# Rearranging the last four units of a fused attention and gated-FFN kernel

## The chip, the cores and the metric

The kernel runs on one core of a Trainium2 chip. The metric is the device time of one execution in microseconds; the median of several runs is compared. All data are float32.

## The reference

Input `x` is 8 x 256 x 512 (2048 tokens of 512). Two pre-norm blocks follow each other:

```python
x = x + attn(layernorm(x), w_qkv, w_o)
x = x + ffn(layernorm(x), weight, bias, centroids, assignments)
```

Attention has 32 query heads and 8 key/value heads of 128, is causal, and adds a bias of `-slope(head) * sqrt(distance)` to the scores. The FFN is one dense layer of 512 x 512 that is masked by token and by column:

```python
dots = softmax(x @ centroids.T / 0.1)     # 64 clusters
hits = dots > 0.01
query_sel = any(hits, axis=1)             # one flag for each token
row_sel = any(hits, axis=0)[assignments]  # one flag for each output column
out = where(query_sel & row_sel, x @ weight.T + bias, 0)
```

The column flags need the hits of every token. So no output can be written before the last token has its hits.

## The kernel before

The 2048 tokens are 16 tiles of 128, in four pairs of sequences (`p`, four tiles each). A unit `u` of the main loop is one sequence of a pair and one key/value head with its four query heads; there are `NU` = 64 units, 16 (`SPP`) for each pair. The loop runs to `u` = 65, since the work is spread over three units: unit `u` makes the scores and the maxima over keys of `u`, the exponentials and sums of `u - 1`, and P @ v and the output projection of `u - 2`.

The order on every engine is written out by hand (a manual schedule): each engine works through its instructions in program order, and a helper such as `av(0)` or `f(1)` puts its instructions on the engines where it is called. These are the helpers that the change touches:

- `scores`, `over_keys`, `over_quadrants` (behind `rows` and `rows_max`): the scores are made with keys on partitions, so maxima and sums over keys need a reduction in DVE (`r`), a transpose on PE (`tp_r`), another reduction (`row`), and two DMAs on the SP queue: `row` to memory and from there, broadcast, to `bc`. `subtract_max` (POOL for the first 1024 columns, DVE for the rest) and `attend` read `bc`.
- `av(i)` is P @ v of unit `u - 2` (two half products, scaled by 1/sum into `oT` by DVE), and behind the second half POOL makes the four sums of `oT` for a Strassen scheme.
- `w(i)` is product `i` of that scheme for the output projection. Products 1, 6, 7 and 4 add up in one bank (`ps_oa`), and each has to be read (by ACT into `snap`, or by DVE) before the next adds into it. The parts in `snap` are added into the residual `x2` on POOL by `flush_adds`, at the start of the next unit. The last unit (`direct`) adds from the bank on DVE.
- `norm(0)` to `norm(3)`: statistics (DVE), square root (ACT), scale and shift (DVE), normalised tile (ACT) of two tiles.
- `f(0)` to `f(3)` are the FFN of a tile `t_ffn`: transposes of the normalised tile and a copy (`xnT`), the product (`ffn_both`: columns 256 to 575 with the 64 logits, and columns 0 to 255), maximum and exponential of the logits, the bias, and the hits, token flag and residual. Tiles 8 to 11 have it in units 62 to 65, tiles 12 to 15 (`last` = 12) behind the loop.

In unit 65 and behind the loop the last four tiles are normalised as their residuals get ready. `hits_any` gathers the hits; `cnt` and `rsel` are the two products that make the column flags of them. Then DVE puts `y` over `x` where the flag is set (`copy_predicated`) tile by tile, and the SP and ACT queues store in turn. Tiles 1, 2 and 3 (`SPLIT`) are done by POOL with a multiplication and an addition. Finished tiles 0 to 7 had been put aside in memory and are loaded again as four transfers of 1 MB (`back`), at the end of unit 63.

Tiles of a pool with a tag share `bufs` buffers: `p_tp` (transposes) has one bank, `p_sc` two, `p_acc` three, `p_long` one for each of its two tags.

Of the kernel before, what the change touches and what calls it, by code (L numbers as in the profile page):

```python
# [14 lines left out]
F32 = mybir.dt.float32  # L15
I32 = mybir.dt.int32
# [5 lines left out]
B, S, H = 8, 256, 512  # L22
# [31 lines left out]
def block_kernel(  # L54
# [463 lines left out]
    def ffn_logits_product(t, w_ffn):  # L518
        lg = p_sc.tile([P, 512], F32, tag="sc", name="lg")
        ffn_product(t, w_ffn, H, NCL, lg)  # L520
        ffn_sb[t] = lg[:, :NCL]

    def ffn_dense(t, w_ffn, chunks=range(NC_H)):
        if 0 in chunks:
            y_sb[t] = [p_acc.tile([P, 512], F32, tag="acc", name="ps_f")]
        ffn_product(t, w_ffn, 0, H, y_sb[t][0], chunks)

    def ffn_both(t, w_ffn):

        second = p_sc.tile([P, 512], F32, tag="sc", name="ps_lg")  # L530
        ffn_product(t, w_ffn, HH, HH + NCL, second)
        first = p_acc.tile([P, 512], F32, tag="acc", name="ps_f")
        ffn_product(t, w_ffn, 0, HH, first)
        ffn_sb[t] = second[:, HH : HH + NCL]
        y_sb[t] = [first[:, :HH], second[:, :HH]]
# [114 lines left out]
    for u in range(NU + 2):  # L650
# [46 lines left out]
        def f(part):  # L697
            if t_ffn is not None:
                if part == 0:
                    ffn_transpose(t_ffn)  # L700
                elif part == 1:
                    ffn_both(t_ffn, w_ffn)
                    ffn_max(t_ffn)
                    ffn_exp(t_ffn)
                elif part == 2:
                    ffn_bias_add(t_ffn, y_late[:, t_ffn % TPP, :] if t_ffn >= first_late else None)
                else:
                    ffn_hits(t_ffn)
                    ffn_qsel(t_ffn)
                    ffn_end(t_ffn)  # L710
# [3 lines left out]
        if more_p and slot in (10, 11):  # L714
            t_norm = (p + 1) * TPP + 2 * (slot - 10)
        elif own and p > 0 and slot in (2, 4) and p < NPAIR - 1:
            t_norm = (p - 1) * TPP + slot - 2
        elif u in (NU - 3, NU - 1):
            t_norm = (NPAIR - 2) * TPP + u - (NU - 3)

# [54 lines left out]
        if bb == 0 and own:  # L775
            qq(1), e(1), max_and_old(), e(2), f(0), av(0), e(6), exp_old(), av(1), more_sums(), rows_max(), f(1), e(7), qq(2)
# [4 lines left out]
        elif u < NU - 1:  # L781
            e(1), qq(4), e(2), max_and_old(), f(0), e(6), av(0), exp_old(), e(7), av(1), f(1), e(5), qq(5)
            f(2), norm(0), e(4), e(3), x(0), w(1), x(1), sum_old(), w(5, 6), norm(1), qq(3), w(2)
            rows(), behind_rows(), w(7, 3), norm(3), w(4)
        elif own:

            max_and_old(), f(0), av(0), exp_old(), av(1), rows_max(), f(1)
            f(2), norm(0), w(1), sum_old(), w(5, 6), norm(1), w(2)
            rows(), subtract_max(u, 0), subtract_max(u, 1)
            f(3), norm(2), w(7)  # L790
            nc.scalar.activation(s_sb[u], s_sb[u], AF.Exp)
            w(3), norm(3), w(4)
        elif bb == 0:
            sum_old(), av(0), av(1), f(0), rows(), f(1), w(1, 5), f(2), w(6, 2, 7, 3, 4), f(3)
        else:
            av(0), f(0), av(1), f(1)
            normalise(norm_stats(last, last + 1), tags=("y", "y"))
            ffn_hits(t_ffn), ffn_qsel(t_ffn)
            w(1), f(2), w(2, 5, 6)
            ffn_transpose(last)  # L800
            w(3)
            found = norm_root(norm_stats(last + 2))
            ffn_transpose(last + 1, "snap")
            w(7)
            norm_write(norm_scale(found))
            ffn_logits_product(last, w_ffn), ffn_logits_product(last + 1, w_ffn)
            w(4)

# [37 lines left out]
        if u == NU - 1:  # L846
# [12 lines left out]
    ffn_dense(last, w_ffn)  # L859
    normalise(norm_stats(last + 3))  # L860
    ffn_max(last), ffn_exp(last)
    ffn_max(last + 1), ffn_exp(last + 1)
    ffn_transpose(last + 2, copy=nc.vector.tensor_copy)
    ffn_transpose(last + 3, "o_s", tp=p_acc.tile([P, 512], F32, tag="acc", name="tpx_late"), copy=nc.vector.tensor_copy)
    ffn_logits_product(last + 2, w_ffn), ffn_logits_product(last + 3, w_ffn)
    ffn_max(last + 2), ffn_exp(last + 2)
    ffn_max(last + 3), ffn_exp(last + 3, work.tile([P, NCL], F32, tag="kT", name="e_last", bufs=2))
    ffn_dense(last + 1, w_ffn, (0, 1))
    for i in range(4):
        ffn_hits(last + i)  # L870
# [5 lines left out]
    nc.vector.tensor_scalar(csel, cnt[:NCL, :P], 0.0, None, ALU.is_gt)  # L876
    rsel = p_tp.tile([P, 512], F32, tag="tp", name="rsel")
    nc.tensor.matmul(rsel, lhsT=csel, rhs=onehot, start=True, stop=True)  # L878
    ffn_dense(last + 1, w_ffn, (2, 3))
# [6 lines left out]
    ffn_end(last - 1), ffn_bias_add(last, y_of(0)), ffn_end(last), ffn_qsel(last + 1)  # L886
    ffn_dense(last + 2, w_ffn)
    rsel_sb = work.tile([P, H], F32, tag="s", name="rsel_sb", bufs=3)
    nc.scalar.copy(rsel_sb, rsel)
    ffn_dense(last + 3, w_ffn)  # L890
    ffn_bias_add(last + 1, y_of(1)), ffn_end(last + 1)
# [5 lines left out]
    n = 0  # L897
    for t in range(NT):
        if t in SPLIT:
            continue  # L900
        p, i = divmod(t, TPP)
        if t >= last + 2:
# [7 lines left out]
        n += 1  # L910
# [23 lines left out]
```

## Time and profile before

| | |
|---|---|
| median of 3 runs | 1436.63 us (1436.61 to 1437.09) |
| profiled execution, its own time | 1438.62 us |
| its span, first to last instruction | 1436.8 us |
| busy: PE / DVE / POOL / ACT | 1404.8 / 928.7 / 877.6 / 372.4 us |
| mean granted clock of TensorE | 0.995 |
| DMA over the span | 190.20 MB, 132 GB/s |

Busy time is an average over the whole span. The change lies in its last 120 us, so the timeline of each engine there counts more than the shares. In a timeline line the columns are start, duration, engine, line of the kernel, operation, output and inputs; the bracket at the end holds the idle time ahead of it on its engine and the instruction that ended it. The timeline merges instructions of one kind. Matmuls in float32 appear as two records each, with weight loads as rows of their own.

### The profile page before, as it was taken

Reading aid. Unit: us, or ns where it says so; the run is one execution under the profiler, and the core shown is the slowest. Engines: PE = TensorE matmul, PEld = TensorE weight load, DVE = VectorE, ACT = ScalarE, POOL = GpSimd, SP = SyncE. Lnnn points to the kernel's source line nnn. Section 1 sums busy time; section 2 is a strip of 40 time slices with the busy share of each in tenths; the row PEclk is TensorE's granted clock in tenths of the full one; section 3 lists DMA queues with packets and bytes.
Section 4 is the critical chain, followed back from the end, with each engine's and each line's share of the span. In section 5 each row is a group of like instructions: output and inputs, shape, how many; then the busy total and the mean of one; then the engine's idle time right before and its main releaser. Section 6 shows DMA issues by size and latency. Waiting matters only on the chain. (4 is left out here: it accounts for less than half of the span.)

```text
span 1436.8 us, 16560 instructions
## 1 busy us (share of the span) xinstructions
PE 1404.8 (98%) x5859; PEld 1082.3 (75%) x5859; DVE 928.7 (65%) x1720; ACT 372.4 (26%) x650; POOL 877.6 (61%) x883
## 2 busy tenths in 40 slices
PE   8899999999999999999999999999999999999986
PEld 7677777767878777777778777787777777777663
DVE  5557656676566665667655666566756676556776
ACT  3222223411232222332213312142222221222332
POOL 6377857767465754667655466566747666466643
PEclk9999999999999999999999999999999999999998
DMA  5235433443242544424243424434323353243243
GB/s 187 94 117 177 132 117 133 147 147 125 96 165 74 176 147 148 162 96 142 101 147 107 171 87 169 168 112 148 132 100 107 132 176 132 90 165 103 91 160 117
DMA packets 87024, 190.20 MB, mean 132 GB/s; under 512 B 11648, under 2 KB 19840, under 8 KB 86944
## 3 DMA queue, kind: packets, MB, share of 16 engines
q1 hardware_dynamic: 85792, 186.67, 37.9%
q10 hardware_dynamic: 864, 1.57, 0.3%
q8 instruction: 47, 0.77, 0.2%
q0 software_dynamic: 288, 0.92, 0.2%
q14 instruction: 33, 0.27, 0.1%
HBM read 176.03 MB, written 13.11 MB: 132 GB/s over the span
## 5 line engine op out<-in xcount | busy, mean ns | idle before, releaser
L423 POOL TENSOR_TENSOR s<-s,bc 128x1024 f32<-128x1024 f32 x64 | 151.7, 2371 | 151.4 <-DMA bc<-row_hbm 151.3
L501 POOL TENSOR_TENSOR x<-x,snap 128x256 f32<-128x256 f32 x189 | 136.0, 735 | 172.1 <-DVE x L489 99.0
L388 DVE TRANSPOSE_TENSOR_REDUCE r<-s 128x32 f32<-128x1024 f32 x128 | 158.0, 1234 | 4.3 <-ACT s L740 4.3
L112 POOL TENSOR_TENSOR o_s<-oT 128x256 f32<-128x256 f32 x64 | 47.7, 745 | 184.3 <-DVE oT L451 178.8
L158 ACT COPY qT<-ps_qa 128x512 f32<-128x512 f32 x128 | 74.7, 583 | 287.4 <-PE ps_qa L145 287.3
L484 ACT COPY snap<-ps_oa 128x256 f32<-128x256 f32 x189 | 70.3, 372 | 274.6 <-PE ps_oa L469 274.6
L469 PE MATMUL ps_oa<-wo,oT 128*128 128x256 f32 x512 | 133.1, 382 | 2.7 <-DVE oT L451 2.7
L740 ACT ACTIVATE s<-s 128x1536 f32<-128x1536 f32 x63 | 93.5, 1484 | 149.3 <-DVE s L426 138.5
L447 PE MATMUL av<-s,v 128*128 128x512 f32 x256 | 130.7, 592 | 0.0
L145 PE MATMUL ps_qa<-xT,wq 128*128 128x256 f32 x512 | 121.1, 379 | 0.8 <-ACT qT L158 0.8
L371 PE MATMUL sc<-qT,kT 128*128 128x512 f32 x256 | 120.3, 592 | 0.0
L145 PEld LDWEIGHTS ps_qa<-xT,wq 128*128 128x128 f32 x512 | 97.1, 190 | 27.8 <-issue 16.0
L373 DVE SCALAR_TENSOR_TENSOR s<-sc,alibi 128x512 f32<-128x512 f32 x128 | 88.0, 691 | 30.8 <-PE sc L371 29.9
L469 PEld LDWEIGHTS ps_oa<-wo,oT 128*128 128x128 f32 x512 | 90.8, 190 | 21.4 <-DVE oT L451 6.1
L379 DVE SCALAR_TENSOR_TENSOR s<-sc,alibi 128x512 f32<-128x512 f32 x64 | 44.3, 692 | 86.5 <-PE sc L377 86.5
L448 PEld LDWEIGHTS av<-s,v 128*128 128x128 f32 x256 | 48.6, 190 | 61.2 <-issue 61.2
L451 DVE TENSOR_TENSOR oT<-av,bc 128x512 f32<-128x512 f32 x128 | 83.9, 682 | 15.1 <-PE av L448 10.5
L389 DVE TRANSPOSE_TENSOR_REDUCE r<-s 128x16 f32<-128x512 f32 x128 | 85.6, 669 | 0.0
L448 PE MATMUL av<-s,v 128*128 128x256 f32 x256 | 76.1, 379 | 0.0
L371 PEld LDWEIGHTS sc<-qT,kT 128*128 128x128 f32 x256 | 48.6, 190 | 33.9 <-issue 28.7
L489 DVE TENSOR_TENSOR x<-x,ps_ob 128x256 f32<-128x256 f32 x64 | 26.9, 421 | 72.9 <-PE ps_ob L469 72.9
L391 DVE TENSOR_TENSOR r<-r 128x16 f32<-128x16 f32 x128 | 69.6, 543 | 4.4
(189 smaller groups left out, 2971.3 us busy)
## 6 DMA issues: line engine op xcount, KB each, us to landing
bc<-row_hbm SPq DMA_DIRECT2D x128, 512.0 KB, 4.9
wq<-in_w_qkv SPq DMA_DIRECT2D x32, 1024.0 KB, 7.8
wo<-in_w_o SPq DMA_DIRECT2D x32, 1024.0 KB, 7.8
alibi<-al_hbm SPq DMA_DIRECT2D x24, 512.0 KB, 8.5
wk<-in_w_qkv SPq DMA_DIRECT2D x16, 512.0 KB, 9.4
wv<-in_w_qkv SPq DMA_DIRECT2D x8, 1024.0 KB, 10.8
x<-in_x SPq DMA_DIRECT2D x16, 256.0 KB, 9.4
al_hbm<-alibi SPq DMA_DIRECT2D x8, 512.0 KB, 9.0
```

Of the source, the lines that this page charges most:

```text
L145: nc.tensor.matmul(bank[:, cols], lhsT=lhsT, rhs=rhs, start=first and j == 0, stop=j == len(mms) - 1, skip_group_check=True)
L371: nc.tensor.matmul(sc, lhsT=kT[:, t0 : t0 + P], rhs=qT[:, hh : hh + 2, t0 : t0 + S], start=True, stop=True)
L373: nc.vector.scalar_tensor_tensor(s[:, hh * S : (hh + 2) * S], sc, D ** -0.5, bias[:, hh : hh + 2, :].rearrange("p h q -> p (h q)"), ALU.mu ...
L388: nc.vector.tensor_reduce(first, s[:, :K0].rearrange("p (j q) -> p j q", q=32), AX.X, op, apply_transpose=True)
L389: nc.vector.tensor_reduce(second, s[:, K0:].rearrange("p (j q) -> p j q", q=32), AX.X, op, apply_transpose=True)
L423: gp(k0, k0, mx, sub)
L447: nc.tensor.matmul(av, lhsT=v[:, i0, vc], rhs=pT[:, hh * S : (hh + 2) * S], start=True, stop=False)
L448: nc.tensor.matmul(av3[:, :, P:S], lhsT=v[:, i0 + 1, vc], rhs=pT[:, K0 + hh * P : K0 + (hh + 2) * P].rearrange("p (h q) -> p h q", h=2), s ...
L451: ve(oT[:, e].rearrange("p k m q -> p k (m q)"), av3, inv[:, hh : hh + 2, :], ALU.mult)
L469: nc.tensor.matmul(bank[:, :HH], lhsT=x[:, e, :], rhs=y[:, e, :], start=first and e == 0, stop=e == 1, skip_group_check=True)
L501: gp(c, c, s, ALU.add)
L740: nc.scalar.activation(s_sb[u - 1], s_sb[u - 1], AF.Exp)
```

## The change

- Unit 61: the statistics of tiles 10 and 11 are taken too (ahead of the third score), and their root and scale follow at its end; the normalised tiles are written in unit 63. The statistics, root and scale of unit 63 are gone.
- Units that have FFN work: `ffn_both` is split in `ffn_second` (with the logits; `f(1)`) and `ffn_first` (`f(1.5)`, which holds the maximum and exponential too). In units of the first kind `rows_max` (or, in unit 64, `rows`) comes between the two.
- Unit 63's hits, token flag and residual (tile 9) move to unit 64. In unit 64 `flush_adds` comes behind product 7; the statistics and root of tiles 12 and 13 come at its end.
- Unit 65: tile 11's first half comes behind the last projection product, with its bias and hits; both transposes of tiles 12 and 13 stand behind product 7; the logits products leave the unit; tile 15 is normalised at its end.
- The four loads of `back` move from the end of unit 63 to the end of unit 64.
- Behind the loop: transposes and logits products of the last four tiles are interleaved, the dense products are cut in chunks and reordered around `cnt` and `rsel`, and the second 1 MB of put-aside tiles (4 to 7) is selected by one `copy_predicated` and stored by one DMA, ahead of the others; the order of the other tiles changes.

```diff
@@ -515,24 +515,27 @@
             nc.tensor.matmul(bank[:, :n], lhsT=xnT_sb[t][:, c, :], rhs=w[:, c, at : at + n],
                              start=c == 0, stop=c == NC_H - 1)
 
-    def ffn_logits_product(t, w_ffn):
-        lg = p_sc.tile([P, 512], F32, tag="sc", name="lg")
+    def ffn_logits_product(t, w_ffn, pool=p_sc, tag="sc"):
+        lg = pool.tile([P, 512], F32, tag=tag, name="lg")
         ffn_product(t, w_ffn, H, NCL, lg)
         ffn_sb[t] = lg[:, :NCL]
 
-    def ffn_dense(t, w_ffn, chunks=range(NC_H)):
+    def ffn_dense(t, w_ffn, chunks=range(NC_H), pool=p_acc, tag="acc"):
         if 0 in chunks:
-            y_sb[t] = [p_acc.tile([P, 512], F32, tag="acc", name="ps_f")]
+            y_sb[t] = [pool.tile([P, 512], F32, tag=tag, name="ps_f")]
         ffn_product(t, w_ffn, 0, H, y_sb[t][0], chunks)
 
-    def ffn_both(t, w_ffn):
+    def ffn_second(t, w_ffn):
 
         second = p_sc.tile([P, 512], F32, tag="sc", name="ps_lg")
         ffn_product(t, w_ffn, HH, HH + NCL, second)
+        ffn_sb[t] = second[:, HH : HH + NCL]
+        y_sb[t] = [None, second[:, :HH]]
+
+    def ffn_first(t, w_ffn):
         first = p_acc.tile([P, 512], F32, tag="acc", name="ps_f")
         ffn_product(t, w_ffn, 0, HH, first)
-        ffn_sb[t] = second[:, HH : HH + NCL]
-        y_sb[t] = [first[:, :HH], second[:, :HH]]
+        y_sb[t][0] = first[:, :HH]
 
     def ffn_max(t):
         lg = ffn_sb[t]
@@ -699,7 +702,9 @@
                 if part == 0:
                     ffn_transpose(t_ffn)
                 elif part == 1:
-                    ffn_both(t_ffn, w_ffn)
+                    ffn_second(t_ffn, w_ffn)
+                elif part == 1.5:
+                    ffn_first(t_ffn, w_ffn)
                     ffn_max(t_ffn)
                     ffn_exp(t_ffn)
                 elif part == 2:
@@ -717,6 +722,8 @@
             t_norm = (p - 1) * TPP + slot - 2
         elif u in (NU - 3, NU - 1):
             t_norm = (NPAIR - 2) * TPP + u - (NU - 3)
+            if u == NU - 3:
+                found_late = norm_stats(t_norm + 2, t_norm + 3)
 
         def norm(part):
             nonlocal found
@@ -773,38 +780,46 @@
                 norm_tile(p + 1, 2 * (slot - 11) + i)
 
         if bb == 0 and own:
-            qq(1), e(1), max_and_old(), e(2), f(0), av(0), e(6), exp_old(), av(1), more_sums(), rows_max(), f(1), e(7), qq(2)
+            qq(1), e(1), max_and_old(), e(2), f(0), av(0), e(6), exp_old(), av(1), more_sums(), f(1), rows_max(), f(1.5), e(7), qq(2)
             if u == 4:
                 onehot_of_columns(asg)
             f(2), norm(0), e(5), e(4), qq(6), e(3), x(0), w(1), x(1), sum_old(), w(5, 6), norm(1), qq(7), w(2)
             rows(), behind_rows(), w(7, 3), norm(3), w(4)
         elif u < NU - 1:
-            e(1), qq(4), e(2), max_and_old(), f(0), e(6), av(0), exp_old(), e(7), av(1), f(1), e(5), qq(5)
+            e(1), qq(4), e(2), max_and_old(), f(0), e(6), av(0), exp_old(), e(7), av(1), f(1), f(1.5), e(5), qq(5)
             f(2), norm(0), e(4), e(3), x(0), w(1), x(1), sum_old(), w(5, 6), norm(1), qq(3), w(2)
-            rows(), behind_rows(), w(7, 3), norm(3), w(4)
+            rows(), behind_rows()
+            if u == NU - 3:
+                found_late = norm_scale(norm_root(found_late))
+            w(7, 3), norm(3), w(4)
         elif own:
 
-            max_and_old(), f(0), av(0), exp_old(), av(1), rows_max(), f(1)
-            f(2), norm(0), w(1), sum_old(), w(5, 6), norm(1), w(2)
+            max_and_old(), f(0), av(0), exp_old(), av(1), rows_max(), f(1), f(1.5)
+            f(2), w(1), sum_old(), w(5, 6), w(2)
             rows(), subtract_max(u, 0), subtract_max(u, 1)
-            f(3), norm(2), w(7)
+            w(7)
+            norm_write(found_late)
             nc.scalar.activation(s_sb[u], s_sb[u], AF.Exp)
-            w(3), norm(3), w(4)
+            w(3), w(4)
+            t_old = t_ffn
         elif bb == 0:
-            sum_old(), av(0), av(1), f(0), rows(), f(1), w(1, 5), f(2), w(6, 2, 7, 3, 4), f(3)
+            sum_old(), av(0), av(1), f(0), f(1), rows()
+            ffn_hits(t_old), ffn_qsel(t_old), ffn_end(t_old)
+            f(1.5), w(1, 5), f(2), w(6, 2, 7)
+            flush_adds()
+            w(3, 4), f(3)
+            found = norm_root(norm_stats(last, last + 1))
         else:
-            av(0), f(0), av(1), f(1)
-            normalise(norm_stats(last, last + 1), tags=("y", "y"))
-            ffn_hits(t_ffn), ffn_qsel(t_ffn)
-            w(1), f(2), w(2, 5, 6)
-            ffn_transpose(last)
-            w(3)
+            av(0), f(0), norm_write(norm_scale(found), tags=("y", "y")), av(1), f(1)
+            ffn_max(t_ffn), ffn_exp(t_ffn)
+            w(1, 2, 5, 6, 3)
             found = norm_root(norm_stats(last + 2))
-            ffn_transpose(last + 1, "snap")
             w(7)
+            ffn_transpose(last, "bc"), ffn_transpose(last + 1, "snap")
             norm_write(norm_scale(found))
-            ffn_logits_product(last, w_ffn), ffn_logits_product(last + 1, w_ffn)
             w(4)
+            normalise(norm_stats(last + 3))
+            ffn_first(t_ffn, w_ffn), f(2), f(3)
 
 
         for dst, src in stores:
@@ -843,7 +858,7 @@
             asg = load_assignments()
         if u == NU - 3:
             y_late = work.tile([P, TPP, H], F32, tag="v", name="y_late", bufs=2)
-        if u == NU - 1:
+        if u == NU:
 
             for i, (tag, pool) in enumerate((("xT", work), ("wq", wpool))):
                 both = []
@@ -856,17 +871,18 @@
 
 
     y_of = lambda i: y_last[i // 2][:, i % 2, :]
-    ffn_dense(last, w_ffn)
-    normalise(norm_stats(last + 3))
+    ffn_logits_product(last, w_ffn, p_long, "aq")
+    ffn_transpose(last + 2, copy=nc.vector.tensor_copy)
+    ffn_logits_product(last + 1, w_ffn)
     ffn_max(last), ffn_exp(last)
+    ffn_transpose(last + 3, "o_s", tp=p_acc.tile([P, 512], F32, tag="acc", name="tpx_late"), copy=nc.vector.tensor_copy)
     ffn_max(last + 1), ffn_exp(last + 1)
-    ffn_transpose(last + 2, copy=nc.vector.tensor_copy)
-    ffn_transpose(last + 3, "o_s", tp=p_acc.tile([P, 512], F32, tag="acc", name="tpx_late"), copy=nc.vector.tensor_copy)
     ffn_logits_product(last + 2, w_ffn), ffn_logits_product(last + 3, w_ffn)
     ffn_max(last + 2), ffn_exp(last + 2)
+    ffn_hits(last)
     ffn_max(last + 3), ffn_exp(last + 3, work.tile([P, NCL], F32, tag="kT", name="e_last", bufs=2))
-    ffn_dense(last + 1, w_ffn, (0, 1))
-    for i in range(4):
+    ffn_dense(last, w_ffn, (0, 1))
+    for i in (1, 2, 3):
         ffn_hits(last + i)
 
 
@@ -874,31 +890,35 @@
     nc.tensor.matmul(cnt[:NCL, :P], lhsT=hits_any, rhs=ones, start=True, stop=True)
     csel = work.tile([NCL, P], F32, tag="oT", name="csel")
     nc.vector.tensor_scalar(csel, cnt[:NCL, :P], 0.0, None, ALU.is_gt)
+    ffn_dense(last + 1, w_ffn, (0,))
     rsel = p_tp.tile([P, 512], F32, tag="tp", name="rsel")
     nc.tensor.matmul(rsel, lhsT=csel, rhs=onehot, start=True, stop=True)
-    ffn_dense(last + 1, w_ffn, (2, 3))
+    ffn_dense(last, w_ffn, (2, 3))
     for i in (2, 3, 0):
         ffn_qsel(last + i)
 
     for i in (2, 3):
         nc.scalar.activation(y_of(i), bias_bc, AF.Copy, scale=ffn_sb[last + i])
         gp(y_of(i), y_of(i), x2[last + i], ALU.add)
-    ffn_end(last - 1), ffn_bias_add(last, y_of(0)), ffn_end(last), ffn_qsel(last + 1)
-    ffn_dense(last + 2, w_ffn)
+    ffn_qsel(last + 1)
+    ffn_dense(last + 1, w_ffn, (1, 2, 3))
     rsel_sb = work.tile([P, H], F32, tag="s", name="rsel_sb", bufs=3)
     nc.scalar.copy(rsel_sb, rsel)
+    ffn_dense(last + 2, w_ffn, pool=p_long, tag="aw")
     ffn_dense(last + 3, w_ffn)
-    ffn_bias_add(last + 1, y_of(1)), ffn_end(last + 1)
     for t in SPLIT:
         xt, yt = back[0][0][:, t, :], back[0][1][:, t, :]
         gp(yt, yt, rsel_sb, ALU.mult)
         gp(xt, xt, yt, ALU.add)
         nc.gpsimd.dma_start(of[ts(t, P), :], xt)
-    n = 0
-    for t in range(NT):
-        if t in SPLIT:
-            continue
+
+    xt, yt = back[1]
+    nc.vector.copy_predicated(xt, rsel.bitcast(I32).unsqueeze(1).to_broadcast([P, TPP, H]), yt)
+    nc.scalar.dma_start(of[PT_TOK : 2 * PT_TOK, :].rearrange("(i p) h -> p i h", p=P), xt)
+    for n, t in enumerate((8, 9, 10, last, 11, last + 1, 0, last + 2, last + 3)):
         p, i = divmod(t, TPP)
+        if t in (last, last + 1):
+            ffn_bias_add(t, y_of(i)), ffn_end(t)
         if t >= last + 2:
             nc.vector.scalar_tensor_tensor(y_of(i), y_sb[t][0], ffn_sb[t], y_of(i), ALU.mult, ALU.add)
         if p < NPAIR - 2:
@@ -907,7 +927,6 @@
             xt, yt = x2[t], y_of(i) if t >= last else y_sb[t]
         nc.vector.copy_predicated(xt, rsel.bitcast(I32), yt)
         (nc.sync if n % 2 == 0 else nc.scalar).dma_start(of[ts(t, P), :], xt)
-        n += 1
 
 
 def kernel(**inputs):
```

## The prediction

> **What bounds the kernel now.** I read the page first (engine shares), then the timeline of TensorE over the last 120 us for its idle stretches, then that of the engine named beside each, then the stretches (granted clock, DMA share) and the end. Units are the loop's `u`; u = 61 to 65 and the code behind the loop lie in 1320 to 1436.8 us. An engine takes its instructions in program order.
>
> ```profile
> PE 1404.8 (98%) x5859; PEld 1082.3 (75%) x5859; DVE 928.7 (65%) x1720; ACT 372.4 (26%) x650; POOL 877.6 (61%) x883
> ```
>
> PE is full nearly everywhere, so a gain is PE idle time removed, PE work taken off the way to the end, or a shorter store phase. The timeline of TensorE (start, us, what, in brackets the idle time ahead and its releaser):
>
> ```profile
> 1344.18 0.27 PE L398 MATMUL tp_r<-ident,r 128*32 128x128 f32 x1 [1.25 <-DVE r L391]
> ...
> 1369.81 0.27 PE L398 MATMUL tp_r<-ident,r 128*64 128x128 f32 x1 [2.00 <-DVE r L391]
> ...
> 1370.98 1.91 PE L469 MATMUL ps_oc<-wo,o_s 128*128 128x256 f32 x4
> 1372.68 1.76 PE L469 MATMUL ps_oa<-wo_t,oT 128*128 128x256 f32 x4
> ...
> 1399.24 1.10 PE L469 MATMUL ps_oa<-wo_t,o_s 128*128 128x256 f32 x4 [1.32 <-DVE x L482]
> ...
> 1415.84 0.40 PE L874 MATMUL cnt<-ones,hits_any 128*64 128x128 f32 x2 [1.31 <-DVE hits_any L565]
> ```
>
> Behind the 2.00 us gap two half products take 1.91 and 1.76 us instead of 1.03. The stretches say why (granted clock third from the end), and the same happened once more in the trace, behind a gap of 1.48 us:
>
> ```profile
> 1371.50:1372.50 1.00, 1.00 (x4) 0.82 (x3) 1.00 (x1) 0.10 (x1) 1.00 (x2) 0.50 0.03 4
> ```
>
> ```profile
> 300.55 1.30 PE L469 MATMUL ps_oa<-wo,oT 128*128 128x256 f32 x4 [1.48 <-DVE oT L451]
> ```
>
> DVE and POOL around the 2.00 us gap:
>
> ```profile
> 1365.07 0.68 DVE L260 BATCH_NORM_STATS2 stats<-x 128x6 f32<-128x512 f32 x1
> ...
> 1366.68 1.21 DVE L388 TRANSPOSE_TENSOR_REDUCE r<-s 128x32 f32<-128x1024 f32 x1
> 1367.82 0.67 DVE L389 TRANSPOSE_TENSOR_REDUCE r<-s 128x16 f32<-128x512 f32 x1
> 1368.52 1.14 DVE L391 TENSOR_TENSOR r<-r 128x16 f32<-128x16 f32 x1
> ```
>
> ```profile
> 1367.29 2.34 POOL L423 TENSOR_TENSOR s<-s,bc 128x1024 f32<-128x1024 f32 x1 [2.41 <-DMA bc<-row_hbm]
> ```
>
> Statistics stand ahead of the reduction that PE waits for, and its last step (0.17 us elsewhere) sits blocked until POOL is done at 1369.6. Last, the end: SP's first store, DVE's last copy, and DMA at its limit between them (last two columns: DMA share, GB/s).
>
> ```profile
> 1422.92 0.34 SPq L909 DMA_DIRECT2D out<-back_xT  x1
> ```
>
> ```profile
> 1431.09 0.72 DVE L908 COPY_PREDICATED x<-rsel,y_alibi 128x512 f32<-128x512 int32 x1
> ```
>
> ```profile
> 1432.00:1434.00 2.00, 0.00 (x0) 0.00 (x0) 0.00 (x0) 0.00 (x0) 0.00 (x0) 0.50 1.03 379
> ```
>
> All output (16 tiles of 256 KB) leaves in 11.3 us from 1423.75. Call R the end of `rsel` (1417.74): the end is R + 19.06. Call W the end of the last half product (1405.96): R is W + 11.78.
>
> **The change, part by part.** Gains are against this execution.
>
> *u = 61.* Two more statistics (4 DVE instructions, 1.61 us as at 1365.07 to 1366.68) come ahead of the third score. DVE idles 1.89 us there for PE (1322.59 to 1324.48): hidden; without that cover they would cost 1.6. The second root finds its table loaded, on an idle ACT (1333.9 to 1335.5): 0.
>
> *u = 62.* The second half product (8 records, 2.16 us) moves ahead of the maxima's transpose, into the 1.25 us gap; its input was copied by 1340.98. It starts at 1342.77, the transpose comes at 1344.93 (maxima ready 1344.03), the first half ends at 1346.77, and the projection starts there, not at 1348.26: **+1.5**. DVE's row reduction came only at 1345.76, so the row DMA stays where it is.
>
> *u = 63.* Without the statistics the reduction starts at 1365.07; two pitches of 1.14 and 0.70 put L391 at 1366.92, 0.37 ahead of POOL; done 1367.1, before PE ends its products (1367.65). The gap goes (2.0) and the half clock with it (8 records of 634 ns for 379, pitch 0.43 for 0.22, some 1.7), and a bit of start-up: **+3.9**. Both table loads (1.28 each) go; the Exp is issued behind two Identities (1.5) and ends near 1372.1 instead of 1375.6. Tile 9's hits leave this unit.
>
> *u = 64.* Those hits (1.63 us on DVE in `ffn_hits`, `ffn_qsel`, `ffn_end`) land between the row reduction and tile 10's maximum. Queued behind them: maximum (0.36), then on ACT exp (0.5) and the first snap copy (0.37), which product 6 waits for, since it adds into the bank. In before this maximum was done at 1381.1 and product 6 at 1383.95 waited for nothing. Counting from u's start T: row done T + 6.9; POOL is still in its two weight sums and four o_s sums until T + 11, and the two-input steps of the hits each wait for a POOL step, as L391 did (1.14 for 0.17) and L426 at 1371.04 (1.70 for 0.68): hits done at T + 10.0, maximum 10.35, exp 10.9, snap 11.25; product 6 would be due at T + 9.6. **-1.6**; unblocked 0, every step blocked by a whole POOL step -2.5. The row's transpose comes 2.16 later; its DMAs don't queue behind 4 MB any more: in before the row write issued at 1380.29 let SP issue the broadcast only at 1389.74, 9.4 us for 1.4. That alone was worth nothing, because PE had tile 11's products to do until 1395.17. But they now leave that place, so without the moved loads the projection would start near 1395 instead of 1393, some 2 us. The loads themselves (4 DMAs on SP, behind the broadcast; 13.6 us to landing) start some 4 us later than before and are needed at R, over 15 us after they land: 0. SP's next work is the stores.
>
> *u = 65.* Out of PE's way to W: tile 11's first half (1.73), two logits products (2.0) and the 1.32 gap (DVE no longer waits there for a root and hits): 5.0. New: ACT has the root of tiles 12, 13 ahead of tile 11's xnT copy. DVE gives its statistics only after tile 10's hits and end: T + 0.54 + 1.63 + 1.61 = T + 3.8; root 0.3, copy 0.6: PE, free at T + 3.0, waits until T + 4.75 (1.7). And the two transposes now follow each other through one bank, with a copy of 0.58 between that stands behind tile 14's root: 1.1. Net with pitches: 17.7 becomes 14.95, **+2.75**. Table loads: root, exp and root again make as many (4) from u = 63 on as before; each finds ACT idle.
>
> *W to R.* PE has less (dense half instead of all), but DVE is the chain: add, statistics, root, scale to W + 2.2; bias add of tile 11 (0.7), its hits and end (1.63) to 4.45; copy of tile 14 (0.65), maximum 12 (0.33), copy 15 (0.6), maximum 13 (0.35) to 6.35; exp 13 to 6.9 frees the bank for logits 15, done 7.9; maximum 15 to 8.36, three hits at 0.63 to 10.25; cnt, then one dense chunk (0.86, where before PE waited 0.38), rsel: W + 12.65. **-0.9**.
>
> *R to the end.* Before, DVE did 4.4 us of sums between R and its first copy at 1422.16. Now the copy of four tiles comes first (2.3 at a pitch of 0.53 to 0.64), so DMA starts near R + 3.2, not R + 6.0. DVE still has some 13.5 us (two `ffn_end` blocked about 0.65 by POOL's sums, as at 1420.42), POOL's third store is issued at R + 13.3: with start 0.8, transfer 0.7 and 1.75 from the last byte to the span's end, R + 17.0. Fed without a hole it would be R + 3.2 + 11.3 + 1.75 = R + 16.2. **+2.0**.
>
> Sum: 1.5 + 3.9 - 1.6 + 2.75 - 0.9 + 2.0 = 7.65.
>
> **The clock.** Gaps of 1.48 and 2.00 us were each followed by 3.4 us at half clock; 1.25, 1.31 and 1.32 were not. The new waits (1.6 and 1.7) lie between. The Trainium skill ("TensorE: Matmul & The Clock Gate", Part 1 and "Why this matters for your kernels") has a free-running window of 3413 ns, which the stretches agree with, but asks only that idle gaps stay below about 3 us. By that rule the new waits cost nothing more: 7.65, or 1429.0. By the rows a gap of that size costs 1.7 when it falls into one window; of two such gaps I count one: 6.0. I take the rows. Neither dropping gives 0, both and one more in the tail -5.1.
>
> The execution took 1438.62 in all for a span of 1436.8; the median without profile is 1436.63. I take the gain off the median: **1430.6**.
>
> **Rivals.**
> A, as summed: 0.52; own range 1428.5 to 1433.
> B, no new wait bites (hits unblocked, no clock drop): 1.5 + 3.9 - 0.1 + 2.75 - 0.9 + 2.0 = 9.15, so 1427.5. For it: u = 62 and 65 have POOL idle at such places. 0.16.
> C, the gap in u = 63 stays: POOL starts before L391, the 0.37 us being no more than the spread of a broadcast (3.5 to 4.4 us to landing). 3.7 of A's gain go: 1434.3. 0.15, of which 0.06 is still faster by over 0.2%.
> E, C and a second clock drop: 1436. 0.08.
> D, slower: half clock through the tail. From W on PE has 64-column products, transposes and waits of 0.7 to 0.8; if the gate counts that as idle, the way to R grows by some 9 (first half, four logits, transposes, dense chunk, cnt, rsel at double) and the 11.2 us of dense work after R, of which DVE's last step waits, by 8. Five of seven windows would take 12: 1442.8. It decides from 9 us on. Against it: in 1409 to 1419, the same mixture, the clock stayed 1.00. 0.09.
> That the change doesn't do what it says: the moved loads alone remove no wait of PE, and table loads are not fewer; both are in A.
>
> **How the numbers follow.** 0.2% is 2.9 us, about what a measurement of this kernel can tell. Faster: A, B and 0.06 of C, 0.74. Same: the rest of C and E, 0.17. Slower: D, 0.09. The range leaves out D and the outer edges: 1426.0 to 1435.5.
>
> **What would show it.** No gap over 1 us at PE in u = 62, and none ahead of the transpose in u = 63; clock 1.00 there. In u = 64 product 6 waiting for a snap copy; in u = 65 the second half waiting for the xnT copy. R near W + 12.6, first store near R + 2.5, end near R + 17. A gap behind L391 in u = 63 or a clock of 0.5 after W would make the prediction wrong.

## The result and the profile after

| | before | changed |
|---|---|---|
| median of ten runs each, first comparison | 1436.2 us | 1432.4 us |
| ratio of the changed kernel to before | | 0.9975, 95% interval 0.9967 to 0.9984 |
| repeated (28 and 17 runs) | 1437.1 us | 1433.1 us; 0.9975, 0.9967 to 0.9983 |
| span of the profiled execution | 1436.8 us | 1430.1 us |

The change makes the kernel 0.25% faster, 3.8 us. The forecast was 6.0.

Where it comes from is best seen by stages, each measured in one profiled execution of each kernel. A unit runs from its first score product (units 62 and 63) or its first P @ v product (64 and 65) to the next one's; W is the start of DVE's last addition from the projection (0.03 us behind the end of the last half product), R the end of `rsel`.

| us | unit 62 | unit 63 | unit 64 | unit 65 to W | W to R | R to the end | sum |
|---|---|---|---|---|---|---|---|
| before | 17.4 | 19.9 | 14.0 | 17.7 | 11.75 | 19.1 | 99.8 |
| changed | 16.35 | 15.9 | 15.2 | 15.3 | 12.8 | 18.4 | 94.05 |
| gain | +1.1 | +3.9 | -1.2 | +2.4 | -1.0 | +0.6 | +5.8 |
| forecast | +1.5 | +3.9 | -1.6 | +2.75 | -0.9 | +2.0 | +7.65 |

The two spans differ by 6.7 us. The other 0.9 lies ahead of unit 62 (it starts at 1336.98 and 1336.05), where the change does nothing until the end of unit 61, and where executions of one kernel differ by more (a second profile of the changed kernel has it at 1339.16).

The lines of the changed kernel that answer to those shown of before are first those of the timeline of TensorE (start, us, what; idle time ahead and its releaser in brackets):

```profile
1343.99 0.27 PE L398 MATMUL tp_r<-ident,r 128*32 128x128 f32 x1
...
1365.63 0.27 PE L398 MATMUL tp_r<-ident,r 128*64 128x128 f32 x1
...
1379.18 1.10 PE L469 MATMUL ps_oa<-wo_t,o_s 128*128 128x256 f32 x4 [0.95 <-ACT snap L484]
...
1388.21 2.42 PE L515 MATMUL ps_lg<-w_ffn,xnT_xnT 128*128 128x320 f32 x8 [1.45 <-ACT xnT_xnT L292]
...
1397.34 0.66 PE L291 MATMUL tpx<-ident,xn 128*128 128x128 f32 x4 [1.09 <-ACT xnT_bc L292]
```

Both transposes that PE had waited for (1.25 and 2.00 us) have no bracket any more. In their place stand three new waits, each for an ACT instruction: for a snap copy, for tile 11's copy, and for the copy between the two transposes. In unit 63, DVE's last step of the reduction comes 0.2 us ahead of POOL's subtraction and takes 0.18 us instead of 1.14:

```profile
1364.92 0.18 DVE L391 TENSOR_TENSOR r<-r 128x16 f32<-128x16 f32 x1
```

```profile
1365.12 2.35 POOL L423 TENSOR_TENSOR s<-s,bc 128x1024 f32<-128x1024 f32 x1 [2.25 <-DMA bc<-row_hbm]
```

In unit 64 DVE has tile 9's hits between the row and tile 10's maximum, and ACT has the exponential ahead of the snap copy (1378.67) that product 6 waits for:

```profile
1375.99 0.71 DVE L568 TENSOR_TENSOR hits_any<-hits_any,e 128x64 f32<-128x64 f32 x1
1376.62 0.21 DVE L572 TENSOR_REDUCE qsel<-e 128x1 f32<-128x64 f32 x1
1376.87 0.98 DVE L581 SCALAR_TENSOR_TENSOR y_late<-y_late,qsel,x 128x512 f32<-128x512 f32 x1
1377.86 0.22 DVE L543 TENSOR_REDUCE cmax<-ps_lg 128x1 f32<-128x64 f32 x1
```

```profile
1378.37 0.31 ACT L553 ACTIVATE e<-ps_lg,cmax 128x64 f32<-128x64 f32 x1 [6.18 <-DVE cmax L544]
1378.58 0.19 ACT L553 ACTIVATION_READ_ACCUMULATOR e<-ps_lg,cmax 128x1 f32 x1
1378.67 0.36 ACT L484 COPY snap<-ps_oa 128x256 f32<-128x256 f32 x1
```

In unit 65 ACT has the root of tiles 12 and 13, which waits for DVE's statistics, ahead of tile 11's copy, for which PE waits 1.45 us:

```profile
1387.39 0.30 ACT L268 ACTIVATE rstd<-mv,eps 128x2 f32<-128x2 f32 x1 [3.67 <-DVE mv L261]
1387.59 0.57 ACT L292 COPY xnT_xnT<-tpx 128x512 f32<-128x512 f32 x1
```

At the end, DVE's part behind R (1411.67), two of POOL's steps beside it, and then the stretches (last two columns: DMA share and GB/s):

```profile
1412.33 2.50 DVE L916 COPY_PREDICATED back_wq<-rsel,back_wq 128x2048 f32<-128x2048 int32 x1 [1.94 <-ACT rsel_sb L906]
...
1417.29 1.44 DVE L581 SCALAR_TENSOR_TENSOR y_kT<-y_kT,qsel,x 128x512 f32<-128x512 f32 x1
...
1420.72 1.88 DVE L581 SCALAR_TENSOR_TENSOR y_kT<-y_kT,qsel,x 128x512 f32<-128x512 f32 x1
...
1426.04 0.72 DVE L928 COPY_PREDICATED x<-rsel,y_alibi 128x512 f32<-128x512 int32 x1
```

```profile
1416.89 1.28 POOL L911 TENSOR_TENSOR back_xT<-back_xT,rsel_sb 128x512 f32<-128x512 f32 x1
...
1420.76 1.27 POOL L911 TENSOR_TENSOR back_xT<-back_xT,rsel_sb 128x512 f32<-128x512 f32 x1
```

```profile
1422.00:1423.00 1.00, 1.00 (x3) 0.19 (x1) 0.97 (x2) 0.00 (x0) 0.92 (x2) 1.00 1.04 377
1423.00:1424.00 1.00, 0.03 (x1) 0.00 (x0) 1.00 (x3) 0.00 (x0) 0.72 (x1) 1.00 0.48 180
```

DVE's first copy waits for ACT (R + 0.66), its last one ends at R + 15.1, and DMA, at its limit up to 1423, has a hole while DVE still works. Each of the two residual steps (1.44 and 1.88 us, 0.75 elsewhere) ends 0.6 us behind one of these POOL steps. In before DMA was full for 3.2 us behind DVE's last copy, and the end came 5.0 us behind that copy; now it comes 3.3 us behind it (3.2 to 3.4 in every later profile of the changed kernel or a version of it), so DVE sets the end.

### The profile page after: what moved, and what is told of

The parts are those of the page before. It is cut to its first block, busy times and chain, and to the rows that moved or that the text cites. A ratio compares the mean times of both kernels' runs of the same rounds, so it can differ in the third digit from the quotient of the medians.

```text
span 1430.1 us, 16553 instructions
## 1 busy us (share of the span) xinstructions
PE 1402.7 (98%) x5859; PEld 1082.0 (76%) x5859; DVE 929.5 (65%) x1717; ACT 372.2 (26%) x650; POOL 877.8 (61%) x883
## 4 chain that ended last, share of the span: by engine, by line
PE 88%; DVE 7%; DMA 2%; issue 1%; POOL 1%; ACT 1%; SPq 0%; ACTq 0%; DVEq 0%; POOLq 0%
PE ps_qa L145 14%; PE ps_oa L469 14%; PE ps_oc L469 7%; PE sc L371 7%; PE ps_qc L145 7%; PE av L447 6%; PE ps_ka L145 4%; PE sc L377 4%; PE ps_ob L469 4%; PE ps_va L145 3%; PE ps_qb L145 3%; PE av L448 3%; PE ps_kc L145 2%; PE ps_vc L145 2%; PE ps_lg L515 2%
```

## The experiments

Each median stands beside that of the kernel before on the same chip. As executions differ by several us ahead of unit 62, what an edit does is read from the stages; the medians decide whether a version is faster.

**The changed kernel again: what its spread goes with.** No edit.

> The changed kernel as it is, to see how its executions spread and what the spread goes with. Theory (clock): the new waits of PE in units 64 and 65 (0.95, 1.45 and 1.09 us) are each followed by a stretch at half clock in some executions and not in others, so that an execution's span goes with its mean granted clock: one stretch of 3.4 us lowers the mean by 0.0012 and costs 1.7 us. Spans from 1428 to 1435 us, with about 1.4 us for each 0.001 of clock, and a median 3 to 5 us below the kernel before. Rival (DMA): the spread comes from the output stores at the end; then it does not go with the clock.

1433.1 us against 1437.1. Over the 27 runs of the changed kernel in both comparisons the span goes with the mean granted clock: at 0.999 one run of 1428.1 us, at 0.998 a median of 1430.2 (6 runs), at 0.997 of 1431.2 (16), at 0.995 of 1433.7 (3), at 0.994 1434.6 (1). That is some 1.1 to 1.3 us for each 0.001, as the first theory had it. The mean is no pure measure of such stretches, though: it also counts the last part of the span, in which PE has no work left and the clock falls to half as well (5.0 us of it in the profile after, 1.8 with tiles 4 to 7 one by one; the difference alone is 0.0011 of the mean). And in the profiled execution the half clock came neither in unit 64 nor in 65. Of all the profiles on record seven have the waits of about 1.0, 1.45 and 1.09 us in these units, and in none of them is the clock halved behind one, so that part of the theory has no support. Two stretches lay in the unchanged part of the loop (near 61 and 1167 us, well ahead of unit 62), and one in the tail:

```profile
1410.00:1411.00 1.00, 1.00 (x2) 0.48 (x2) 0.90 (x6) 0.41 (x2) 0.00 (x0) 0.50 0.00 0
```

It followed no long gap, but several small waits (0.75 and 0.59 us the longest). There W to R took 13.7 us instead of 12.8. The profile after has one stretch as well, near 302, behind a gap of 1.30 us (four records of this kind take 1.03 us at full clock):

```profile
300.05 1.30 PE L469 MATMUL ps_oa<-wo,oT 128*128 128x256 f32 x4 [1.30 <-DVE oT L451]
...
302.88 1.91 PE L469 MATMUL ps_oa<-wo_t,o_s 128*128 128x256 f32 x4
```

So the spread goes with the clock, and the stretches seen come from elsewhere than the new waits: three from parts of the loop that no edit touches, one from the tail.

**Tile 9's hits later.**

```diff
-            ffn_hits(t_old), ffn_qsel(t_old), ffn_end(t_old)
-            f(1.5), w(1, 5), f(2), w(6, 2, 7)
+            f(1.5), w(1, 5), f(2)
+            ffn_hits(t_old), ffn_qsel(t_old), ffn_end(t_old)
+            w(6, 2, 7)
```

> The changed kernel, but in unit 64 tile 9's hits, flag and residual come behind the bias add of tile 10 instead of ahead of tile 10's maximum. Theory (queue on DVE and ACT): product 6 waits 0.95 us because its bank is read by a snap copy that stands on ACT behind tile 10's exponential, whose maximum stands on DVE behind those hits. Then the wait goes, unit 64 takes 14.0 to 14.3 us instead of 15.2 (from the first P @ v product to the next unit's), and the span falls by about 1.2. Rival (POOL): the o_s sums are what is late; then product 6 waits for POOL and unit 64 stays near 15.2.

1432.8 us against 1437.1 (ratio 0.9966, 0.9953 to 0.9978). Unit 64 takes 14.05 us and product 6 waits for nothing: the cause is the order on DVE and ACT, not POOL's sums. But the gain went on to the next wait, in the timeline of TensorE:

```profile
1387.49 4.04 PE L515 MATMUL ps_lg<-w_ffn,xnT_xnT 128*128 128x320 f32 x8 [2.01 <-ACT xnT_xnT L292]
```

It grew from 1.45 to 2.01, and this time the half clock followed (these eight products took 4.04 us, and 2.42 in the changed kernel), so that unit 65 took 17.6 us instead of 15.3. In this execution units 64 and 65 together take 31.6 us, and 30.6 in the changed kernel; the forecast fall of the span by 1.2 did not come.

**The root of tiles 12 and 13 later.**

```diff
-            found = norm_root(norm_stats(last, last + 1))
+            found = norm_stats(last, last + 1)
...
-            av(0), f(0), norm_write(norm_scale(found), tags=("y", "y")), av(1), f(1)
+            av(0), f(0), norm_write(norm_scale(norm_root(found)), tags=("y", "y")), av(1), f(1)
```

> The changed kernel, but the root of tiles 12 and 13 is issued in unit 65 behind tile 11's xnT copy instead of at the end of unit 64. Theory (order on ACT): the second half product of tile 11 waits 1.45 us only because its xnT copy stands on ACT behind that root. Then this wait goes, W (the end of the last half product) comes 1.2 to 1.5 us earlier after the start of unit 65 (15.3 to about 14), and the span falls by as much. Rival: the scaled P @ v of unit 63 is late on DVE anyway, so that the wait moves to the first projection product and the gain is under 0.5.

1430.6 us against 1437.1 (0.9960, 0.9945 to 0.9974). The wait is gone, unit 65 takes 13.6 us: 1.7 less, a little more than expected. Tile 11's copy only stood in the wrong place on ACT.

**The big loads a slot earlier.** The four transfers back at the end of unit 63 (`if u == NU - 1` instead of `if u == NU`).

> The changed kernel, but with the four 1 MB loads back at the end of unit 63. Theory: the row of unit 63 (4 KB, then its broadcast) lands behind 4 MB, some 9 us for the first hop instead of 1.4, and the broadcast lands 1.5 to 2.5 us after DVE wants it in unit 65; unit 65 gets longer by 0 to 2 us, for it has only tile 11's second half to do meanwhile. Rival (the loads are what the change is about): 5 us or more are lost. Second rival (nothing): the broadcast was hidden in the kernel before and is hidden here too, within 0.3.

1431.6 us against 1437.1 (0.9962, 0.9949 to 0.9974). The second rival holds: unit 65 takes 15.3 us with and without. The traffic is as described, in the DMA issues of SP:

```profile
1374.48 0.32 SPq L407 DMA_DIRECT2D row_hbm<-row  x1
1383.72 0.33 SPq L416 DMA_DIRECT2D bc<-row_hbm  x1
```

The broadcast is issued 9.2 us behind the row instead of 1.4, and DVE waits for it:

```profile
1387.49 0.69 DVE L451 TENSOR_TENSOR oT<-av,bc 128x512 f32<-128x512 f32 x1 [1.00 <-DMA bc<-row_hbm]
```

But PE has 1.45 us of waiting for tile 11's copy ahead of the projection, and the 1.00 disappears in it. Whether the move is worth something once that wait is gone was not tried.

**Tile 11's residual step later.**

```diff
-            ffn_first(t_ffn, w_ffn), f(2), f(3)
+            ffn_first(t_ffn, w_ffn), f(2), ffn_hits(t_ffn), ffn_qsel(t_ffn)
+            t_old = t_ffn
...
+    ffn_end(t_old)
     ffn_dense(last + 1, w_ffn, (0,))
```

> The changed kernel, but tile 11's residual step (`ffn_end`, 0.67 to 0.75 us of DVE) comes behind `csel` instead of ahead of tile 14's copy. Theory: from W to R DVE is the chain (its copies, maxima and hits follow each other), so the way from W to R falls from 12.8 us by about 0.7. Rival (ACT and the logits banks): logits 15 waits for exponential 13 to free its bank, so the chain shortens by under 0.3.

1430.1 us against 1435.5 (0.9961, 0.9948 to 0.9975; 4 runs). W to R falls from 12.8 to 12.0: DVE is the chain there. R to the end rises from 18.4 to 19.1: the step moves the flags, and with them POOL's additions, which DVE's later steps wait for. Of 0.8 gained 0.7 come back.

**A second `rsel` for ACT.**

```diff
     nc.tensor.matmul(rsel, lhsT=csel, rhs=onehot, start=True, stop=True)
+    rsel2 = p_sc.tile([P, 512], F32, tag="sc", name="rsel2")
+    nc.tensor.matmul(rsel2, lhsT=csel, rhs=onehot, start=True, stop=True)
...
-    nc.scalar.copy(rsel_sb, rsel)
+    nc.scalar.copy(rsel_sb, rsel2)
```

> The changed kernel with the flags' product made twice, the second time into a bank of its own that only ACT's copy for POOL reads. Theory (DVE waits for ACT's read of the same bank): DVE's first copy starts 0.05 to 0.1 us behind R instead of 0.66. As DVE's 14.4 us behind it are what the last store waits for, the way from R to the end falls by about 0.5; PE's extra 1.1 us is hidden, and POOL starts 1 us later. Rival (the loads or the queue are what it waits for): the first copy stays at R + 0.66.

1431.0 us against 1435.5 (0.9968, 0.9957 to 0.9979). DVE's first copy comes at R + 0.04 and is released by PE, where ACT released it in the changed kernel; so it did wait for ACT's read of that bank:

```profile
1412.47 2.49 DVE L918 COPY_PREDICATED back_wq<-rsel,back_wq 128x2048 f32<-128x2048 int32 x1 [1.68 <-PE rsel L895]
```

But the end doesn't move by the 0.5 that was forecast: 18.4 us behind R, last copy at R + 15.0. The residual step of tile 12 now takes 2.01 us instead of 1.44: what DVE wins at the front it waits for POOL. (In this profile two windows in a row ran at half clock ahead of R, and W to R took 15.3 us.)

**Tiles 4 to 7 one by one.** The single copy and DMA are left out; the loop over the other tiles begins with 4, 5, 6, 7.

> The changed kernel, but tiles 4 to 7 are selected and stored one by one (four copies, four stores of 256 KB), still ahead of the others. Theory (behind R DVE sets the end, not DMA): the first store is issued near R + 1.4 instead of R + 3.2, and yet the way from R to the end stays within 0.4 us of 18.4. Rival A (DMA sets the end, as the forecast's 16.2 us without a hole had it): 1.5 us or more shorter. Rival B (one large DMA is what helps): 0.6 us or more longer.

1430.2 us against 1435.5 (0.9964, 0.9952 to 0.9976). The first store is issued at R + 1.4 instead of R + 3.2, and yet R to the end is 18.4 us, the last copy at R + 15.1: nothing changes. When DMA starts is of no account as long as DVE is late.

**The four edits at once** (hits, root, residual step, and the transposes of tiles 12 and 13 on either side of product 7).

```diff
-            w(1, 2, 5, 6, 3)
-            found = norm_root(norm_stats(last + 2))
-            w(7)
-            ffn_transpose(last, "bc"), ffn_transpose(last + 1, "snap")
+            w(1, 2, 5, 6, 3)
+            ffn_transpose(last, "bc")
+            found = norm_root(norm_stats(last + 2))
+            w(7)
+            ffn_transpose(last + 1, "snap")
```

> The changed kernel with four of its waits taken away at once: tile 9's hits behind tile 10's bias add, the root of tiles 12 and 13 behind tile 11's copy, the transposes of tiles 12 and 13 on either side of product 7, and tile 11's residual step behind `csel`. Theory (each wait has its own cause and they add up): unit 64 14.05 us (15.2 to 15.4 in the changed kernel), unit 65 12.5 to 13 (15.3), W to R 12.1 (12.8); together 4 us below the changed kernel, a median near 1428.5, and fewer stretches at half clock in these units. Rival (one wait takes the place of another): the scaled P @ v of unit 63 is late on DVE, and unit 65 stays above 14.

1427.15 us against 1435.5 (0.9940, 0.9928 to 0.9953). Unit 64 14.05, unit 65 13.0, W to R 12.0, R to the end 19.1: 90.2 in all, 3.9 less than the changed kernel. The waits add up once they are all gone. (The transposes on either side of product 7 had no run of their own.)

**Before, with the early statistics alone.** Statistics in unit 61, root and scale at its end, `norm_write` in unit 63, nothing else.

> The kernel before, with one part of the change alone: statistics, root and scale of tiles 10 and 11 are taken in unit 61 and only the normalised tiles are written in unit 63. Theory: this part is the 3.9 us that unit 63 lost (19.9 to 15.9 us): the reduction that PE waits for comes 1.6 us earlier, the 2.00 us gap goes, and with it the half clock behind it. So unit 63 takes 15.9 to 16.1 us, and the median falls by 2.2 (where an execution has no half clock there) to 3.9 us. Rival: without the moved loads the broadcast of unit 63's row is late in unit 65, and 2 us or more come back there (unit 65 19.7 us or more instead of 17.7).

1437.1 us against 1437.1 (1.0003, 0.9992 to 1.0014): nothing. Neither theory had this. Unit 63 does take 15.9 us. Unit 64 takes 18.6 instead of 14.0, in the timeline of TensorE:

```profile
1374.80 0.27 PE L398 MATMUL tp_r<-ident,r 128*64 128x128 f32 x1 [3.65 <-DVE r L391]
```

The transpose of unit 63's sums stands ahead of tile 10's product there, and the sums are behind tile 9's hits on DVE, whose steps now meet POOL's weight sums:

```profile
1368.91 1.34 DVE L565 TENSOR_TENSOR hits_any<-hits_any,e 128x64 f32<-128x64 f32 x1
```

Behind this wait the clock is halved (the next eight products take 4.01 us instead of 2.32), as it is behind that of unit 63 in before. Units 63 and 64 together: 34.5 us, and 33.9 before. It takes the other edits of the change (hits in unit 64, transpose behind the first product) to keep the gain: 31.2.

Two other units are shorter in this profile, though nothing was changed in them: 65 (see below) and 62, which takes 16.3 us instead of 17.4. There POOL's subtraction starts behind DVE's last step of the reduction, since its broadcast comes later, and PE waits for nothing:

```profile
1341.20 0.18 DVE L391 TENSOR_TENSOR r<-r 128x16 f32<-128x16 f32 x1
```

```profile
1342.02 2.86 POOL L423 TENSOR_TENSOR s<-s,bc 128x1024 f32<-128x1024 f32 x1 [2.22 <-DMA bc<-row_hbm]
```

In before POOL started first (1341.66), and the same step of DVE, from 1342.42, took 1.61 us. So the 1.25 us wait of unit 62 in before depends on when a broadcast lands, and need not be there in every execution.

**Before, with the product cut in two alone.** `ffn_both` split, and `f(1), rows_max(), f(1.5)` in unit 62.

> The kernel before, with one part of the change alone: the FFN product is cut in two and the transpose of the maxima comes between the halves where a unit of the first kind has both (unit 62). Theory: unit 62 falls from 17.4 to 16.0 to 16.4 us, and no other unit changes by more than the half clock does; the median falls by about 1.1. Rival: the row of maxima reaches POOL later and unit 63 loses what unit 62 gains.

1435.3 us against 1437.1 (0.9984, 0.9974 to 0.9993). Unit 62 takes 16.1 us. The rival has no support: unit 63's wait of 1.84 us is that of before (2.00). By chance this profile shows what the half clock behind it is worth, since here none followed: a half product there takes 1.03 us, not 1.91.

```profile
1364.89 0.27 PE L398 MATMUL tp_r<-ident,r 128*64 128x128 f32 x1 [1.84 <-DVE r L391]
...
1365.96 1.03 PE L469 MATMUL ps_oc<-wo,o_s 128*128 128x256 f32 x4
```

Unit 63 takes 18.0 us and unit 64 15.7 (two waits of 1.03 and 1.22 for ACT and DVE), together 33.7; with the half clock they took 33.9. In this pair of profiles, then, PE waits for the other engines for about as long as it otherwise loses to the clock.

**Another division behind R**, on the changed kernel, with tiles 4 to 7 one by one.

```diff
-    SPLIT = (1, 2, 3)
+    SPLIT = (1, 2)
...
-    for i in (2, 3, 0):
+    for i in range(4):
         ffn_qsel(last + i)
...
-    for i in (2, 3):
+    for i in range(4):
+        if i == 2:
+            nc.scalar.copy(rsel_sb, rsel)
         nc.scalar.activation(y_of(i), bias_bc, AF.Copy, scale=ffn_sb[last + i])
         gp(y_of(i), y_of(i), x2[last + i], ALU.add)
-    ffn_qsel(last + 1)
...
+    for n, t in enumerate((4, 5, 6, 7, 3, 8, 9, 10, last, 11, last + 1, 0, last + 2, last + 3)):
...
-        if t in (last, last + 1):
-            ffn_bias_add(t, y_of(i)), ffn_end(t)
-        if t >= last + 2:
+        if t >= last:
```

> The changed kernel with another division of the work behind R: tiles 12 and 13 are finished as tiles 14 and 15 are (bias times flag on ACT, residual added on POOL, one DVE instruction), and in return POOL's own tiles are 1 and 2 instead of 1, 2 and 3; tiles 4 to 7 one by one. Theory (DVE sets the end, above all by its two residual steps of 1.4 and 1.9 us that wait for POOL[...]): DVE's last copy comes near R + 13 instead of R + 15.1, DMA has no hole left, and the end comes at R + 16 to R + 16.6 instead of R + 18.4. Rival (POOL sets the end): POOL has two more additions of 1.25 us ahead of its stores, and the end stays within 0.5 of R + 18.4.

1430.6 us against 1437.1 (0.9954, 0.9940 to 0.9968; 4 runs). R to the end is 16.2 us instead of 18.4; DVE's last copy ends at R + 13.0. Each of tiles 12 and 13 now takes one instruction that doesn't wait for POOL:

```profile
1418.85 0.72 DVE L917 SCALAR_TENSOR_TENSOR y_kT<-ps_f,qsel,y_kT 128x512 f32<-128x512 f32 x1
...
1420.85 0.73 DVE L917 SCALAR_TENSOR_TENSOR y_kT<-ps_f,qsel,y_kT 128x512 f32<-128x512 f32 x1
```

POOL's own part ends earlier as well (its last store is issued at R + 10.6 instead of R + 12.35), so the run doesn't separate the two engines. The end still lies 3.2 us behind DVE's last copy.

**The four edits and the other division together.**

> The kernel that had four waits taken away (tile 9's hits later, the root of tiles 12 and 13 later, transposes apart, tile 11's residual step behind `csel`), with the other division of the work behind R as well. Theory: the two add up, since they lie in different stages: units 64 and 65 14.05 and 13.0 us, W to R 12.0, R to the end 16.3 to 17.2 instead of 19.1; 2 to 2.8 us below the version with the four waits taken away, a median near 1425. Rival: tile 11's residual step behind `csel` now stands where POOL's additions start, and gives back 1 us or more.

1424.85 us against 1437.1: ratio 0.9913, 0.9901 to 0.9925. Stages: 16.2, 15.9, 14.05, 13.0, 12.0, 16.1; 87.3 us, 6.7 less than the changed kernel and 12.5 less than before. The rival is wrong: the other division also takes away the steps to which the moved residual step gave its 0.7 back. This version beats both kernels.

## Why the prediction was right, and where it was off

- **Unit 61, hidden.** Right. In the changed kernel the statistics fill 1321.6 to 1323.2, and DVE still idles 0.28 us for the third score behind them. PE waits for DVE nowhere in this unit.
- **Unit 62, +1.5.** Measured +1.1; alone, on the kernel before, +1.3. The projection does start 1.5 us earlier behind the unit's start (9.8 instead of 11.3), as the working had it; of this 0.3 are lost at the transpose of the sums, whose reduction stands on DVE behind a bias addition that waits for ACT's exponential. How much of the 1.25 us wait an execution of before has depends on a broadcast, as the early statistics alone showed.
- **Unit 63, +3.9.** Measured +3.9. The margin of 0.37 us to POOL was 0.2, and held: unit 63 took 15.9 us in every profile with the early statistics. Rival C did not happen. But the term was priced alone, and the experiments show that it can't be: alone it comes back whole in unit 64. Only the 2.3 of both units together (3.9 - 1.6) was a quantity; it measured 2.7.
- **Unit 64, -1.6.** Measured -1.2, by the mechanism named: hits, maximum, exponential, snap, product 6. Moving the hits removed it.
- **Unit 65, +2.75.** Measured +2.4; the two waits of 1.7 and 1.1 are 1.45 and 1.09.
- **The loads.** The working said that without the move the projection would start some 2 us later. It starts at the same time: this price is wrong, because the 1.45 us wait covers it. It also said that in before the late broadcast cost nothing. The three profiles of the old order of unit 65 speak against that: DVE gets its broadcast 5.4, 4.2 and less than 2.5 us behind the unit's start (before, cut product alone, early statistics alone), and the unit takes 17.7, 16.5 and 16.3 us. The 1.32 us wait of product 6 for DVE stands only in the first. That the one is the other's cause was not tried by itself.
- **W to R, -0.9.** Measured -1.0. DVE is the chain, as assumed; shortening it by the residual step shortened the stage by 0.8.
- **R to the end, +2.0.** This is the step that failed: +0.6. DVE's 13.5 us measured 15.1 from R to the last copy. Of these 1.6, 0.66 are the wait for ACT's read of the same bank, which was not thought of, and about half of the rest is in the two residual steps, 1.44 and 1.88 us, not 1.4 each. (The sum itself was a little off: 13.5 and the three terms behind it, 0.8, 0.7 and 1.75, make 16.75, not 17.0; the tail measured 3.3.) And the stage is set by DVE and POOL together, so that neither an earlier first copy nor an earlier first store moves it, while taking work off both moved it by 2.3.
- **The clock, -1.7.** The forecast counted one stretch of half clock. The profiled execution has none in these units, and neither have the six others with the same waits. The working had read that gaps of 1.48 and 2.00 us bring it and those up to 1.32 don't; but before has another gap of 1.48 us, at 60.65, with no half clock behind it. By the rows of all traces a gap of this size may or may not bring it: 1.30 us did (in the profile after, near 300), 2.49 did not. The rule of the Trainium skill ("TensorE: Matmul & The Clock Gate", "Why this matters for your kernels"), gaps below about 3 us, is too lenient here: half clock followed single gaps of 1.30 to 2.51 us. So the rows were the better guide, but not as a threshold, and their price for the old gap in unit 63 may be too high: with and without half clock units 63 and 64 took 33.9 and 33.7 us (one profile each).
- **The sum.** 7.65 without the clock measured 5.8; 1.4 of the difference is the stage behind R. That 5.8 lies so near the forecast 6.0 is luck: the 1.7 taken off for a stretch of half clock, which did not come, stands in for terms that were priced too high. The medians differ by 3.8 to 4.0. What lies between 5.8 and 3.8 stays open. The only profile of before is of one of its longer executions (1438.6 us, against medians of 1436.2 to 1437.1), with a wait in unit 62 that the early statistics alone had not, and the latest broadcast in unit 65. And how often the half clock falls into either kernel, single profiles don't give. Of rival D something is real: in two of the eleven profiles with the changed tail the way from W to R ran partly at half clock, and lost 0.9 and 2.5 us.

## What to carry to other kernels

A wait that is taken away goes to the next late instruction in some engine's order, so a gain is priced over two or three stages together, and the orders of the in-order engines are followed instruction by instruction: here a root ahead of a copy and a residual step ahead of a maximum cost 1.2 to 1.7 us each, and the version that moved both, with two more, kept the gain. Where the end is a store phase, find out which engine feeds it by taking work off that engine; an earlier first store is worth nothing while the last one is late. Where a change of a few us is judged, compare stages from profiles as well as medians: a part of the loop that no edit touches moved by as much as the gain.

## What the runs showed of the hardware

- The clock of TensorE was halved for some 3.4 us behind single gaps of 1.30, 1.47, 1.48, 2.00, 2.01, 2.51 and 3.65 us, but not behind others of 1.48, 1.71, 1.80, 1.84 and 2.49: the gap's size alone doesn't decide. In one profile (`rsel` twice) it stayed halved for two such windows in a row, 6.8 us, behind waits of 0.75 and 0.58.
- DVE instructions with two inputs in SBUF took longer beside a busy POOL again and again: `hits_any` 0.71 and 1.34 us instead of 0.23, the residual steps 1.44 to 2.01 instead of 0.75. So did one with a single tensor and a factor for each row, the scaling of the exponentials (`e`): 1.08 instead of 0.26. Copies under a flag that lies in PSUM did not (0.62 us from start to start beside a busy POOL), nor did the step with one input in PSUM (0.73).
- DVE's first read of a PSUM bank was held until ACT's read of the same bank had ended, 0.6 us; with a second copy of the data in another bank the wait was gone. The profile puts the wait down to ACT's instruction; whether the hardware needs it, these runs don't show.
